# Reading and turning the weights beside the first group's order, on one core

## The chip, the cores and the metric

The kernel runs on one core of one Trainium2 chip. The metric is the time of one execution on the device in microseconds (us); for the kernel before it is the median of three runs. One further execution was recorded by the hardware profiler; all durations of single instructions are from it. The engines are named as the profile names them: PE (matrix products; PEld is its loading of weights), DVE (vector), ACT (activation functions), POOL (GpSimd) and SP (here it issues the DMA transfers). An activation function is looked up in a table set; when the next function isn't in the set that is loaded, an ACT_TABLE_LOAD stands before it.

## The reference

128 graphs of 64 nodes with 128 features go through four graph layers, each with a residual and a layer norm followed by a ReLU in front. Cut to what matters:

```python
h = relu(layernorm(x));  x = x + L0(h, adj)   # edge filters from a Gaussian basis of the edge weight
h = relu(layernorm(x));  x = x + L1(h, adj)   # hyperbolic attention over the neighbours
h = relu(layernorm(x));  x = x + L2(h, adj)   # normalised adjacency, one weight
h = relu(layernorm(x));  x = x + L3(h, adj)   # mean of messages, then an update weight

# L0, for the nodes j that i is joined with
g  = exp(coeff * (e[i, j] - offsets)**2)              # 64 offsets
Wf = (ssp(g @ W1.T + b1) @ W2.T + b2) * A[i, j]       # ssp: softplus - ln 2
y  = sum_j (h @ Wa.T)[j] * Wf * A[i, j]
L0 = ssp(y @ Wd1.T + bd1) @ Wd2.T + bd2
# L1 uses W, b_lin, att_w1, att_b1, att_w2, att_b2, mlp_w1, mlp_b1, mlp_w2, mlp_b2; its bias is
hyp_bias = proj(tanh(|b_lin|) * b_lin / |b_lin|)
# L2 uses W, b; L3 uses W_msg, W_upd
```

About a quarter of the edges are there, each with a weight from 0.05 to 5.

## The kernel before

The graphs are worked on in 16 groups of eight. A group lies in four pairs; the two graphs of a pair share the 128 partitions. Seven stages make a group: `load` (x and the adjacency), `order` (the nodes are sorted by their number of neighbours, the adjacency is brought into that order, and for every node its neighbours are put into slots, as zeros and ones in the tile `oh`), `layer0`, `layer1_nodes`, `layer1_edges`, `rest1` (the rest of layer 1) and `rest2` (layers 2 and 3, and the store). The edges are worked on by slot: two blocks of 512 slots and one of 264 for each pair, which are the shapes 128x1024 and 128x528 in the profile (two graphs side by side).

The order of the instructions on PE, DVE, ACT and POOL is laid down by a planner in the program, the class `Weave`. Every stage is a generator (a stream); `yield on(engine, ...)` ends a step and says on which engine the next one begins, which buffers of a ring it takes, after which events, and under which table set of ACT ("log" holds Exp and Ln, "silu" holds Silu and Tanh). The planner has its own estimate of each instruction's duration (`about`, line 785). It picks, of the streams that could begin within 0.05 us of the earliest on that engine, the one with the smallest key; the key is the stream's rank (2 x group + the stage's due time, in the last lines of `sparse_stack`) plus a number from the table `LATE` (line 808), one number for each step of each kind of stream. An instruction on these four engines is issued in the order in which the planner came to it, and each engine's queue is in order. The table sets are asked for in a loop outside the streams, with `preload_act_table_set`, first of all "log". SP is not in this order; transfers that wait for nothing go out in the order of the calls.

Small results on PE go to one PSUM bank, the ring "sm" (one buffer); the edge products go to "big" (three buffers). The order of a group needs "sm" for a chain of steps: two products into the counts of nodes with more neighbours, then x in the new order, the adjacency turned twice, its running count, and beside them the transposed h and its product with Wa, which gives `rf`.

Ahead of the weave, in plain program order, stand the constants and the weights (lines 999 to 1155). The helper `weight_t` (line 1067) reads a weight into a room, turns it on PE through "sm" and copies it out on DVE. The rooms come from `raw_tile` (line 991) and alternate between two tiles, e1 and e2, so that a read has to wait until the turn two before it has been done. The bias of layer 1 is computed with Sqrt and Tanh on ACT. The last of it is the message weight, whose two halves are turned and multiplied with the update weight. Since these instructions come first in the program, those of PE come first in PE's queue too; DVE's first instructions of `order` lie between those of the weights.

```python
    def raw_tile():
        name = f"e{1 + len(raws) % 2}"
...
    def transposed(src, dst):
        ps = psm.tile([P, 512], F32, name="sm", tag="sm")
        T.transpose(ps[:, :P], src, ident)
        V.tensor_copy(dst, ps[:, :P])
```

In the profile nearly all instructions have line 849, where the planner's helper issues them, so they are told apart by the names of their tiles: `e` with `ident` is a weight being turned, `e` with `w1T` and `ex` with `w2T` are layer 0's edge products, `ex<-big` is an Exp and `ex<-ex` the Ln after it, `hbn` is the bias, `oh` the slots of the order, `va` the edge weights in slots.

Of the kernel before, what the change touches and what calls it, by code (L numbers as in the profile page):

```python
# [11 lines left out]
F32 = mybir.dt.float32  # L12
U32 = mybir.dt.uint32
I32 = mybir.dt.int32
# [6 lines left out]
NP = 4  # L21
# [763 lines left out]
def about(engine, op, args, kw):  # L785
# [14 lines left out]
    if engine == ACT:  # L800
# [8 lines left out]
    "attention": (0, 3.75),  # L809
    "coefs_of": (2.5, 0, -0.25),  # L810
    "coefs_of2": (2.5,),
    "duo": (4, 4.25),
    "duo2": (0, 3.5, -1.5),
    "filter_of": (1.75, 3.5, 0.25, -0.75, 0, -2.25),
    "filter_of2": (-3.75, 3.5, 0, 4.5, -2.5),
    "layer1_edges": (0, 0, 0, -3),
    "layer1_nodes": (-2.25, 0, 0, 0, 0, 4.5, 0, 4.25, 1.75, 0, 0, 0, 0, 0, 3.5, 0.5, 0, 0, 0, 0, 0,
        0, 0, 0, -1.5, 0, 0, 0, 0, -3.25, 0, 0, 0, 0, 0, 0, -0.5, 0, 0, 0, 0, 0, 0, 3, 0, 0, 3),
    "neighbours": (-0.5, -2),
    "neighbours2": (3.5,),  # L820
    "one_minus_z": (-1.5,),
    "order": (0, 0, -2.25, 0, 0, 0, 4.25, 3.25, 0, -2, 0, 1.75, 0, 2.25, 0, 0, 1.75, 0, 6, -2.25),
    "product_with_h": (0, 2.5),
    "rest1": (0, 0, 0, -3.75, 0, 0, 0, 1, 0, -3.25, 0, 0, 0, 0, -0.5, -2, 0, 0, 0, 0, 0, 0, -1.25),
    "rest2": (0, 0, 0, 0, 0, 0, 0, 0, 0, 0, 0, -3.75, 0, 2, 0, 2.75, 0, 0, 0, 0, 3.5, 0, 0, 0, 0, 0,
        0, 0, 1),
    "rows": (1.25, -2.75),
    "rows2": (1.75, -0.25),
    "scores_of": (0.75, 0, -1.75, -0.5),
    "scores_of2": (0, -1.25),  # L830
    "squares": (2,),
    "squares2": (0, 2.25),
# [38 lines left out]
class Weave:  # L871
# [18 lines left out]
    def add(self, gen, rank=None, tail=False):  # L890
        rank = self.now.rank if rank is None else rank
        self.streams.append(Stream(gen, self.now.t if self.now else 0.0, rank, tail))

# [69 lines left out]
def sparse_stack(ctx: ExitStack, tc: tile.TileContext, ins, out: bass.AP, flag):  # L963
# [25 lines left out]
    raws = []  # L989

    def raw_tile():

        name = f"e{1 + len(raws) % 2}"
        raws.append(dense.tile([P, NP, N], F32, name=name, tag=name))
        return raws[-1].rearrange("q p n -> q (p n)")[:, 0:P]

# [30 lines left out]
    tri = raw_tile()  # L1027
# [14 lines left out]
    for c, blocks in enumerate(BLOCKS):  # L1042
        at = OFFS[c]
        for k, r0, n, k0 in blocks:
            ki = edge.tile([P, 1024], I32, name="ex", tag="ex", bufs=3)
            G.iota(ki[:, 0:k * n].rearrange("q (n k) -> q n k", n=n), [[0, n], [1, k]], base=k0 - 128,
                   channel_multiplier=0)
            V.tensor_copy(slot_k[:, at:at + k * n], ki[:, 0:k * n])
            V.tensor_copy(slot_r[:, at:at + k * n].rearrange("q (n k) -> q n k", n=n),
                          bl(ident2[:, r0:r0 + n], k))  # L1050
            at += k * n
# [11 lines left out]
    def transposed(src, dst):  # L1063
        ps = psm.tile([P, 512], F32, name="sm", tag="sm")
        T.transpose(ps[:, :P], src, ident)
        V.tensor_copy(dst, ps[:, :P])

    def weight_t(ap, name, dst=None):

        raw = raw_tile()  # L1070
        nc.sync.dma_start(out=raw, in_=ap)
        if dst is None:
            dst = const.tile([P, P], F32, name=name)
        transposed(raw, dst)
        return dst


    w1raw = raw_tile()
    nc.sync.dma_start(out=w1raw[:, 0:NG], in_=ins["L0_gnn_W1"])
    nc.sync.dma_start(out=w1raw[:, NG:P], in_=ins["L0_gnn_W1"])  # L1080
    w1T = const.tile([P, P], F32, name="w1T")
    transposed(w1raw, w1T)


    b1 = column("L0_gnn_b1")
    bound = const.tile([P, 1], F32, name="bound")
    V.tensor_scalar(w1raw[:, 0:NG], w1raw[:, 0:NG], 0.0, None, ALU.max)
    V.tensor_reduce(bound, w1raw[:, 0:NG], AX.X, ALU.add)
    V.tensor_tensor(bound, bound, b1, ALU.add)
    waT = weight_t(ins["L0_gnn_Wa"], "waT")  # L1090
    wd1T = weight_t(ins["L0_gnn_Wd1"], "wd1T")
    bd1 = column("L0_gnn_bd1")
    wd2T = weight_t(ins["L0_gnn_Wd2"], "wd2T")
    w2T = weight_t(ins["L0_gnn_W2"], "w2T")

    b2s = column("L0_gnn_b2")
    ps = psm.tile([P, 512], F32, name="sm", tag="sm")
    T.matmul(ps[:, 0:1], lhsT=w2T, rhs=nln2[:, 0:1], start=True, stop=True)
    V.tensor_tensor(b2s, ps[:, 0:1], b2s, ALU.add)
    bd2s = row("L0_gnn_bd2")  # L1100
    ps = psm.tile([P, 512], F32, name="sm", tag="sm")
    T.matmul(ps[:, :P], lhsT=nln2, rhs=wd2T, start=True, stop=True)
    V.tensor_tensor(bd2s, ps[:, :P], bd2s, ALU.add)


    wlinT = weight_t(ins["L1_gnn_W"], "wlinT")
    attT = const.tile([P, 2 * P], F32, name="attT")
    weight_t(ins["L1_gnn_att_w1"][:, P:2 * P], None, attT[:, 0:P])
    weight_t(ins["L1_gnn_att_w1"][:, 0:P], None, attT[:, P:2 * P])
    ab1 = column("L1_gnn_att_b1")  # L1110
    hab2 = const.tile([P, 1], F32, name="hab2")
    nc.sync.dma_start(out=hab2, in_=ins["L1_gnn_att_b2"].partition_broadcast(P))
    V.tensor_scalar(hab2, hab2, 0.5, None, ALU.mult)
    aw2 = const.tile([P, 1], F32, name="aw2")
    nc.sync.dma_start(out=aw2, in_=ins["L1_gnn_att_w2"].rearrange("o d -> d o"))
    aw2b = const.tile([P, N], F32, name="aw2b")
    V.tensor_scalar(aw2b, ones[:, 0:N], aw2, None, ALU.mult)
    m1aT = weight_t(ins["L1_gnn_mlp_w1"][:, 0:P], "m1aT")
    m1bT = weight_t(ins["L1_gnn_mlp_w1"][:, P:2 * P], "m1bT")
    mb1 = column("L1_gnn_mlp_b1")  # L1120
    m2T = weight_t(ins["L1_gnn_mlp_w2"], "m2T")
    mb2 = row("L1_gnn_mlp_b2")


    hb = row("L1_gnn_b_lin")
    hb2 = raw_tile()
    hbn = const.tile([P, 4], F32, name="hbn")
    V.tensor_tensor(hb2, hb, hb, ALU.mult)
    V.tensor_reduce(hbn[:, 0:1], hb2, AX.X, ALU.add)
    V.tensor_scalar(hbn[:, 0:1], hbn[:, 0:1], MIN_NORM2, None, ALU.max)  # L1130
    S.activation(hbn[:, 0:1], hbn[:, 0:1], AF.Sqrt)
    S.activation(hbn[:, 1:2], hbn[:, 0:1], AF.Tanh)
    V.tensor_scalar(hbn[:, 1:2], hbn[:, 1:2], MAXNORM, None, ALU.min)
    V.reciprocal(hbn[:, 2:3], hbn[:, 0:1])
    V.tensor_tensor(hbn[:, 1:2], hbn[:, 1:2], hbn[:, 2:3], ALU.mult)
    V.tensor_scalar(hb, hb, hbn[:, 1:2], None, ALU.mult)
    V.tensor_tensor(hb2, hb, hb, ALU.mult)
    hby2 = const.tile([P, 1], F32, name="hby2")
    V.tensor_reduce(hby2, hb2, AX.X, ALU.add)


    w2g = const.tile([P, P], F32, name="w2g")
    nc.sync.dma_start(out=w2g, in_=ins["L2_gnn_W"])
    b2g = row("L2_gnn_b")

    wupd = const.tile([P, 2, P], F32, name="wupd")
    nc.sync.dma_start(out=wupd, in_=ins["L3_gnn_W_upd"].rearrange("(s d) u -> d s u", s=2))
    wsu, wru = (const.tile([P, P], F32, name=n) for n in ("wsu", "wru"))
    for k, dst in enumerate((wsu, wru)):
        raw, rawT = (raw_tile() for _ in range(2))  # L1150
        nc.sync.dma_start(out=raw, in_=ins["L3_gnn_W_msg"][k * P:k * P + P, :])
        transposed(raw, rawT)
        ps = psm.tile([P, 512], F32, name="sm", tag="sm")
        T.matmul(ps[:, :P], lhsT=rawT, rhs=wupd[:, 1, :], start=True, stop=True)
        V.tensor_copy(dst, ps[:, :P])
# [185 lines left out]
    def load(g, st):  # L1341
        yield on(DVE, "x", "adj")
        x = st["x"] = pers.tile([P, NP, D], F32, name="x", tag="x")
        adj = st["adj"] = pers.tile([P, NP, N], F32, name="adj", tag="adj", bufs=5)
        gs = slice(2 * NP * g, 2 * NP * (g + 1))
        nc.sync.dma_start(out=adj, in_=adj_d[gs].rearrange("(p b) i j -> (b i) p j", b=2))
        nc.sync.dma_start(out=x, in_=x_d[gs].rearrange("(p b) i d -> (b i) p d", b=2))
        st["x_used"], st["adj_used"] = w.token("x"), w.token("adj")
        w.now.t += 5
        w.event("load", g)  # L1350

    def order(g, st):
# [31 lines left out]
        def normed_x():  # L1384
# [11 lines left out]
            yield on(POOL)  # L1396
# [8 lines left out]
            yield on(PE, "sm")  # L1405
# [34 lines left out]
        for c in range(3):  # L1440
            for at, k, r0, n in blocks_of(c):
                yield on(DVE)
# [26 lines left out]
    def layer0(g, st):  # L1469

        yield on(DVE, "ys", after=prior(("order", g), ("layer0", g - 1), ("va1", g - 2)))
# [139 lines left out]
    def layer1_nodes(g, st):  # L1611


        yield on(PE, "sm", "a0", "a1", after=prior(("layer0", g), ("nodes", g - 1)))
# [58 lines left out]
        def product_with_bias():  # L1673
            yield on(POOL, after=[("n2", g)])
# [403 lines left out]
    def rest2(g, st):  # L2078

        yield on(PE, "sm", after=prior(("rest1", g), ("rest2", g - 1)))  # L2080
# [122 lines left out]
    with tc.manual_schedule(engines={E.Activation, E.PE, E.DVE, E.Pool}):  # L2203
        for g in range(GROUPS):
# [53 lines left out]
```

## Time and profile before

| | |
|---|---|
| median of 3 runs | 2149.32 us (2148.49 to 2150.37) |
| the profiled execution | 2152.3 us, of which its span 2150.5 |
| busy over the span | PE 1826.5 (85%), DVE 1832.9 (85%), ACT 1671.5 (78%), POOL 369.7 (17%) |
| mean granted clock of PE | 0.941 of full |
| table loads on ACT | 87, 111.6 us |
| first matmul of the first group's order | 36.20 us |
| stores of the groups 0 and 9 | 489.2 and 1579.4 us |

The span is cut into 40 slices of 53.8 us each; a digit is the busy share of an engine in a slice, in tenths.

```profile
## 2 busy tenths in 40 slices
PE   3767989898999989898999989898999989896773
DVE  4448889899999989899999989899999999887752
ACT  1968787979879797979879797979879797985541
PEclk9988999999999999999999999999999999998775
DMA  2000000000000000000000000000000000000000
```

PE and DVE are at 8 or 9 tenths from the fifth slice on and fall off in the last four. The DMA engines do next to nothing after the first slice.

### The profile page before, as it was taken

The numbers are of one execution on the slowest core, as the hardware profiler recorded it, in microseconds if no ns is written. First come the engines' busy times: TensorE is split into PE (matmuls) and PEld (weight loads), VectorE is DVE, ScalarE is ACT, GpSimd is POOL, SyncE is SP. The second block draws the span as 40 slices with busy tenths as digits, with TensorE's granted clock in tenths as the row PEclk, the third lists the DMA queues.
The fourth block names the chain that finished last, engine by engine and source line by source line (L and its number), as shares of the span: only waits on it lengthen the run. The fifth ranks groups of instructions, "written<-read, shape, count | busy, mean of one in ns | idle before, by whom it ended". The sixth has DMA issues, their size and how long they took to land.

```text
span 2150.5 us, 32066 instructions
## 1 busy us (share of the span) xinstructions
PE 1826.5 (85%) x11223; PEld 873.5 (41%) x11223; DVE 1832.9 (85%) x4829; ACT 1671.5 (78%) x3385; POOL 369.7 (17%) x362
## 2 busy tenths in 40 slices
PE   3767989898999989898999989898999989896773
PEld 2223333443444444443444444443444444433342
DVE  4448889899999989899999989899999999887752
ACT  1968787979879797979879797979879797985541
POOL 1000101122120212122120212222130212202121
PEclk9988999999999999999999999999999999998775
DMA  2000000000000000000000000000000000000000
GB/s 52 5 0 6 1 6 1 1 6 8 6 8 6 8 6 8 1 6 8 6 8 6 8 6 8 1 6 8 6 8 1 8 1 6 1 1 6 5 1 12
DMA packets 29532, 13.95 MB, mean 6 GB/s; under 512 B 10544, under 2 KB 29360, under 8 KB 29360
## 3 DMA queue, kind: packets, MB, share of 16 engines
q1 hardware_dynamic: 29360, 11.80, 2.1%
q8 instruction: 90, 1.47, 0.3%
q14 instruction: 82, 0.67, 0.1%
HBM read 7.61 MB, written 4.19 MB: 5 GB/s over the span
## 4 chain that ended last, share of the span: by engine, by line
PE 41%; ACT 31%; DVE 22%; issue 4%; DMA 1%; POOL 0%; SPq 0%; DVEq 0%; ACTq 0%; POOLq 0%
PE big L849 29%; PE sm L849 9%; ACT ex L849 9%; ACT e L849 5%; DVE va L849 4%; ACT ra L849 4%; PE sl L849 4%; ACT n L849 3%; DVE oh L849 3%; DVE ex L849 2%; DVE ah L849 2%; DVE y L849 2%; ACT va L849 2%; ACT L849 2%; ACT th L849 1%
## 5 line engine op out<-in xcount | busy, mean ns | idle before, releaser
L849 PE MATMUL big<-ex,w2T 128*128 128x512 f32 (+1 forms) x768 | 328.5, 553 | 41.3 <-ACT ex L849 35.0
L849 PE MATMUL big<-e,w1T 64*128 64x512 f32 (+1 forms) x768 | 205.3, 635 | 57.2 <-ACT e L849 52.6
L849 ACT ACTIVATE ex<-big,c_L_gnn_att_b 128x1024 f32<-128x1024 f32 (+1 forms) x192 | 183.3, 968 | 78.0 <-PE big L849 77.4
L849 DVE SCALAR_TENSOR_TENSOR ex<-big,c_L_gnn_b,ra 128x1024 f32<-128x1024 f32 x128 | 163.8, 1280 | 67.8 <-PE big L849 55.6
L849 PEld LDWEIGHTS big<-ex,w2T 128*128 128x128 f32 x768 | 131.2, 190 | 215.7 <-ACT ex L849 93.0
L849 ACT ACTIVATE ex<-big,c_L_gnn_b 128x1024 f32<-128x1024 f32 (+1 forms) x192 | 184.6, 978 | 43.9 <-PE big L849 43.6
L849 PE MATMUL big<-va,U 64*128 64x512 f32 (+1 forms) x768 | 184.7, 558 | 31.8 <-DVE va L849 31.6
L849 PE MATMUL big<-va,a 64*128 64x512 f32 (+1 forms) x768 | 185.5, 579 | 10.3 <-DVE two L849 4.3
L849 PE MATMUL sl<-ex,aw2b 128*64 128x512 f32 (+1 forms) x768 | 180.7, 549 | 8.4 <-ACT th L849 4.5
L849 ACT ACTIVATE ra<-big 128x528 f32<-128x528 f32 (+1 forms) x192 | 167.3, 884 | 17.7 <-PE big L849 17.0
L849 ACT ACTIVATE ex<-ex 128x1024 f32<-128x1024 f32 (+1 forms) x192 | 175.6, 924 | 0.9
L849 DVE TENSOR_REDUCE y<-ex 128x128 f32<-128x1024 f32 x128 | 155.1, 1212 | 0.8
L849 POOL TENSOR_TENSOR k_r<-k_r,exp 128x4 f32<-128x4 f32 x32 | 47.5, 1484 | 580.4 <-DVE k_r L849 568.7
L849 ACT ACTIVATE th<-sl,hab 128x512 f32<-128x512 f32 (+1 forms) x192 | 118.1, 615 | 37.0 <-PE sl L849 35.2
L849 PE MATMUL big<-slot_r,Sx 64*128 64x512 bf16 (+1 forms) x1152 | 137.4, 343 | 0.0
L849 PEld LDWEIGHTS big<-e,w1T 64*128 64x128 f32 x768 | 69.4, 205 | 155.6 <-ACT e L849 65.2
L849 ACT ACTIVATE va<-va,sr 128x512 f32<-128x512 f32 (+1 forms) x192 | 122.5, 649 | 9.0 <-DVE va L849 9.0
L849 PE MATMUL big<-oh,pqs 64*64 64x512 bf16 (+1 forms) x1152 | 122.8, 347 | 0.0
L849 ACT ACT_TABLE_LOAD x87 | 111.6, 1283 | 2.2 <-PEq L2246 0.7
L849 DVE COPY_PREDICATED va<-slot_r,big 128x1024 f32<-128x1024 uint16 (+1 forms) x96 | 106.6, 1111 | 5.3 <-PE big L849 5.1
L849 DVE TENSOR_TENSOR va<-oh,adjT 128x1024 f32<-128x1024 bf16 (+6 forms) x160 | 103.6, 697 | 5.7 <-ACT va L849 4.9
L849 DVE TENSOR_TENSOR oh<-pos,slot_k 128x2048 bf16<-128x2048 bf16 (+6 forms) x128 | 107.7, 849 | 0.2
(470 smaller groups left out, 3799.6 us busy)
## 6 DMA issues: line engine op xcount, KB each, us to landing
x<-in_x_dram SPq DMA_DIRECT2D x16, 256.0 KB, 2.9
out_dram<-v SPq DMA_DIRECT2D x16, 256.0 KB, 2.3
adj<-in_adj_dram SPq DMA_DIRECT2D x16, 128.0 KB, 2.3
e<-in_L_gnn_mlp_w_dram SPq DMA_DIRECT2D x3, 64.0 KB, 1.8
wupd<-in_L_gnn_W_upd_dram SPq DMA_DIRECT2D x1, 128.0 KB, 5.8
e<-in_L_gnn_Wd_dram SPq DMA_DIRECT2D x2, 64.0 KB, 2.9
e<-in_L_gnn_W_dram SPq DMA_DIRECT2D x2, 64.0 KB, 1.8
e<-in_L_gnn_att_w_dram SPq DMA_DIRECT2D x2, 64.0 KB, 1.8
```

The source lines that it names most:

```text
L849: return f(*args, **kw)
```

## The change

The weights of the layers are no longer read and turned ahead of the weave. Four streams with rank -10 do it inside: `slots_ranks` (the slot tables that the order compares with), `weights0` (layer 0), `weights1` (layer 1 and its bias, with one stream `turned_from` for each of its six turns) and `weights2` (layers 2 and 3, after the events "weights1" and "bias1"). The rooms are now twelve halves of six tiles that later stages use, each for one weight, and for layer 3 a tile of four rooms; no read waits for another turn. The single numbers (columns and rows) are still read ahead. The turns take "sm" as a ring. Stages wait for events: the order for "wa" and "weights0" (at the steps that use them) and for "slots"; `layer0` for "weights0", `layer1_nodes` for "weights1", its product with the bias for "bias1", `rest2` for "weights2". The bias is computed with Ln, Exp and Exp under the table set "log", and Tanh under "silu", in place of Sqrt, Tanh and a reciprocal. The table LATE has other numbers throughout, and entries for the new streams. The diff, with the table and some renamed declarations cut:

```diff
 LATE = {
-    "attention": (0, 3.75),
+    "attention": (0, -0.5),
...
+    "slots_ranks": (3.5, 0, 4.75),
+    "turned_from": (3.5,),
+    "weights_of": (-3,),
...
+    def wait(self, us):
+        self.now.t += us
...
-    raws = []
-    def raw_tile():
-        name = f"e{1 + len(raws) % 2}"
-        raws.append(dense.tile([P, NP, N], F32, name=name, tag=name))
-        return raws[-1].rearrange("q p n -> q (p n)")[:, 0:P]
+    rooms = [(name, k) for name in ("e2", "e4", "bR", "rt", "rs", "mask", "e1") for k in range(2)]
+    def raw_tile():
+        name, k = rooms.pop(0)
+        if k == 0:
+            raw_tile.last = dense.tile([P, NP, N], F32, name=name, tag=name)
+        return raw_tile.last.rearrange("q p n -> q (p n)")[:, P * k:P * k + P]
...
+    def turned(raw, dst):
+        yield on(PE, "sm")
+        ps = psm.tile([P, 512], F32, name="sm", tag="sm")
+        T.transpose(ps[:, :P], raw, ident)
+        yield on(DVE)
+        V.tensor_copy(dst, ps[:, :P])
+        w.release("sm")
...
+    def weights0():
+        yield on(DVE)
+        w1raw = raw_of(ins["L0_gnn_W1"], ins["L0_gnn_W1"])
+        raw = {n: raw_of(ins["L0_gnn_" + n]) for n in ("Wa", "Wd2", "W2", "Wd1")}
+        w.wait(5)
+        yield from turned(raw["Wa"], waT)
+        w.event("wa")
+        yield from turned(w1raw, w1T)
...
+        yield from turned(raw["W2"], w2T)
+        ps = yield from product(w2T, nln2[:, 0:1], 1)
+        V.tensor_tensor(b2s, ps, b2s, ALU.add)
+        yield from turned(raw["Wd2"], wd2T)
+        ps = yield from product(nln2, wd2T, P)
+        V.tensor_tensor(bd2s, ps, bd2s, ALU.add)
+        yield from turned(raw["Wd1"], wd1T)
+        w.event("weights0")
...
+    def weights1():
+        yield on(DVE)
...
+            w.add(turned_from(raw_of(ap), dst))
...
-    S.activation(hbn[:, 0:1], hbn[:, 0:1], AF.Sqrt)
-    S.activation(hbn[:, 1:2], hbn[:, 0:1], AF.Tanh)
...
-    V.reciprocal(hbn[:, 2:3], hbn[:, 0:1])
...
+        yield on(ACT, table="log")
+        act(hbn[:, 1:2], hbn[:, 0:1], AF.Ln)
+        act(hbn[:, 0:1], hbn[:, 1:2], AF.Exp, scale=0.5)
+        act(hbn[:, 2:3], hbn[:, 1:2], AF.Exp, scale=-0.5)
+        yield on(ACT, table="silu")
+        act(hbn[:, 1:2], hbn[:, 0:1], AF.Tanh)
...
+        w.event("bias1")
...
+    def weights2():
+        yield on(DVE, after=[("weights1",), ("bias1",)])
+        nc.sync.dma_start(out=w2g, in_=ins["L2_gnn_W"])
+        nc.sync.dma_start(out=wupd, in_=ins["L3_gnn_W_upd"].rearrange("(s d) u -> d s u", s=2))
+        room = wide.tile([P, NP, D], F32, name="w3", tag="w3")
...
+            yield from turned(raws[2 * k], raws[2 * k + 1])
+            ps = yield from product(raws[2 * k + 1], wupd[:, 1, :], P)
+            V.tensor_copy(dst, ps)
+        w.event("weights2")
...
+        for stream in (slots_ranks, weights0, weights1, weights2):
+            w.add(stream(), -10)
         for g in range(GROUPS):
```

## The prediction

> **What bounds the kernel now.** I read the page first, and from it only the forty slices: the first slice has PE 3 and ACT 1, the fifth is the first in which PE stands at 9, and the last four fall away. So there is a start-up, a long even middle and a drain. Next I asked for the busy time by stage, with cuts at the first matmul of the first group's order (36.2 us), its first edge weights (51.8) and its first layer-0 sum (136.5).
>
> ```profile
> core 0: us, PE busy (x) PEld busy (x) DVE busy (x) ACT busy (x) POOL busy (x), PEclk, DMA share, GB/s
> 0.00:36.20 36.20, 8.91 (x21) 4.41 (x22) 12.72 (x63) 4.25 (x5) 5.20 (x26) 1.00 0.29 69
> 36.20:51.80 15.60, 8.33 (x63) 6.17 (x62) 9.57 (x21) 2.51 (x5) 3.56 (x4) 1.00 0.06 18
> 51.80:136.50 84.70, 58.96 (x244) 22.25 (x245) 38.97 (x59) 79.40 (x86) 0.00 (x0) 0.92 0.01 3
> 400.00:1800.00 1400.00, 1271.27 (x8072) 605.38 (x8070) 1307.89 (x3440) 1182.57 (x2426) 264.06 (x235) 0.98 0.02 6
> ```
>
> In the middle (last row) DVE is busy 93%, PE 91%, ACT 84%; the change takes no instruction out of it. In the first 36 us nothing is busy for more than a third. In the third stage ACT is busy 94%, PE 70%, DVE 46%. The chain of waits shows who owns the first stage: from 13.76 us, when the first adjacency has landed and DVE works on it, the chain follows PE's twelve transposes and four products of weights, with a bias computation between, before the order's own matmul:
>
> ```profile
> 13.76 0.29 DVE o L849
> ...
> 34.17 0.49 PE sm L849
> 34.68 0.30 DVE e L849
> 35.03 0.81 PE sm L849 x2
> 35.86 0.30 DVE wru L849
> 36.20 0.60 PE sm L849 x2
> 36.83 0.43 DVE o L849
> ```
>
> DVE has done its share of the order (the row pos from ident and degs) at 16.25; PE gets to it at 36.20, because PE's queue is in order and the weights stand in it. What fills ACT in the third stage is in the timeline of ACT:
>
> ```profile
> 29.69 1.28 ACT L849 ACT_TABLE_LOAD   x1
> 30.99 0.20 ACT L849 ACTIVATE hbn<-hbn 128x1 f32<-128x1 f32 x1
> ...
> 128.18 1.28 ACT L849 ACT_TABLE_LOAD   x1
> 129.47 1.12 ACT L849 ACTIVATE ex<-big,c_L_gnn_b 128x1024 f32<-128x1024 f32 x1
> 130.61 1.28 ACT L849 ACT_TABLE_LOAD   x1
> 131.90 1.06 ACT L849 ACTIVATE ex<-ex 128x1024 f32<-128x1024 f32 x1
> 132.86 1.00 ACT L849 ACTIVATE ra<-big 128x1024 f32<-128x1024 f32 x1
> 133.89 2.57 ACT L849 ACT_TABLE_LOAD   x2
> ...
> 167.53 0.20 ACT L849 ACTIVATE nn<-nn 128x8 f32<-128x8 f32 x1
> 167.76 0.21 ACT L849 ACTIVATE rr<-nn 128x8 f32<-128x8 f32 x1
> ```
>
> Between an Exp (ex from big) and the Ln after it (ex from ex) stands a table load, and another before the next Exp. After the pair at 133.89, which the program asks for itself, Ln and Exp follow each other without one (167.53, 167.76: Ln, Exp). The groups of ACT in this stage count 23 loads, 29.5 us, mean 1283 ns; less the two asked for, 21 are the alternation. Its cause, by the order in the trace: the program's own load of the set with both functions stands at 0.72 us, and the Tanh of the bias brought another set at 29.69; nobody asked for the joint set again until 133.89.
>
> **The start.** Removed from the front of PE's queue: everything before 36.20. Added: the same turns, in the weave, beside the order. I cost it in three terms.
>
> First, when the adjacency lands. Before, 15 transfers are issued ahead of it on SP, about 0.47 us apart; the issue is at 8.01, DVE uses it at 13.76, 5.7 later. After, 11 columns and rows and 12 weight loads are called ahead of it, since the weight streams have rank -10 and the load -6: eight more, 8 x 0.47 = 3.8. So 13.8 + 3.8 = 17.5 us; bounds 13.8 (SP takes it earlier) and 20 (transfers also queue on each other: the row loads took 3.6 to 5.7). DVE's share is 16.25 - 13.76 = 2.5: PE can begin the order at 20.0, 16.2 before 36.2.
>
> Second, the order's chain itself, from its first matmul to the first edge weights: 36.20 to 51.88, 15.7 us, unchanged.
>
> Third, what the turns put between. Layer 0 and layer 1 need 11 transposes and two products, each of which holds the one small PSUM bank ("sm") that the order uses too. A round, from 23.00 to 23.87, is 0.86 us; 11 x 0.86 and the two products (0.8 and 1.18) make 11.4 us. In time, all of it could lie before 20.0; but the queue is laid by a plan that thinks weights and adjacency are there at 4 or 5 us, so only three or four rounds come first. Of the other nine or ten, one fits where DVE computes between the order's first two matmul steps (1.3 us) and two or three beside the 6.3 us in which DVE writes the eight blocks of oh. That leaves some 5.5 on the path: 5.5 x 0.86 = 4.7. Bounds: none (0) and all (11.4).
>
> Sum: 20.0 + 15.7 + 4.7 = 40.4 instead of 51.9: 11.5 us saved. With all bounds bad: 22.5 + 15.7 + 11.4 = 49.6, 2 saved; with all good: 16.3 + 15.7 = 32, 20 saved.
>
> What is queued behind the new waits: the DVE instructions on hab and aw stand near the front of DVE's manual queue as before and wait for a transfer landing near 8 us; nothing urgent is behind them then. Layer 0's wait for the first weights ends before its other wait, the order's oh, unless the plan puts Wd1 late. The slot tables (3.5 us of DVE from 8.7 to 12.8) lie ahead of the adjacency in either kernel. The waits of the layer-1 nodes for the second weights and of the mlp bias product for the bias come 80 us later. The turns for layer 3 (two transposes, two products, 3.4 us of PE and DVE) now come after the bias, near the end of the first layer 0, where PE is under half busy (136 to 160 us); I take them at 0, at most 3.4. Their consumer, rest2 of group 0, ends at 489 us. SP is in order too, and its loads of x wait for PE; if it put the loads of these weights behind one, PE would stand at their transposes, for the 2 to 5 us of a load at the least. They need nothing but room, so I expect them early.
>
> **The tables.** The bias's Sqrt, Tanh and reciprocal become Ln, two Exp and, under the silu set, Tanh. Outside the plan no ACT function is left that could change the set, so the joint set loaded first stays through the first layer 0, and the 21 loads go. The Tanh falls between the two loads at 133.89, behind which ACT idles 5.5 us before the first nodes: its 0.2 is hidden.
>
> Two rules of the Trainium skill must be weighed here. In the trace the load at 130.61 begins 0.02 after the Exp has ended, and the Ln at 131.90 follows 0.01 after the load: 1.31 us a switch, 21 x 1.31 = 27.5. "ScalarE: Activation LUTs", in What ACT_TABLE_LOAD costs, has a load of 1283 ns, which the trace confirms, and a drain of 1380 besides, 2.66 in all: 21 x 2.66 = 56 us, more than the stage's ACT time leaves room for (79.4 - 56 = 23, while the activations alone sum to 49.9). The row decides. The other speaks against the change: "ScalarE activation tables: per-element evaluation and per-set limits", in Table sets in the compiler and the runtime, says loads are placed per block by the greedy longest run. By that, a run of Exp and Ln would get one load for both, and a forgotten set would cost 1.3 once; this program's rows show 21 instead, so here the set kept is the one last asked for, and what restores the joint set ends the alternation. If I misread that, the loads stay (a rival below).
>
> ACT's 79.4 shrink to 49.9. What is late next is PE: 58.96 busy, of which some 4.5 are slow clock (the four w2T matmuls at 73.20 took 3.78 us at a granted 0.50, at 98.88 1.98 at 1.00), so about 54.5. With the busiest engine at 85%, less than the middle's 93% because one group alone fills and drains here, the stage takes 54.5 / 0.85 = 64.1 instead of 84.7: 20 us saved. Bounds: PE at 75% gives 72.7 (12 saved); above, the 27.5 of the loads.
>
> **The order found anew** changes the keys by which the plan breaks ties, in all sixteen groups. No row tells its sign. From the stores of groups 0 and 9 (489.2 and 1579.4) a group takes 121.1 us, and with DVE at 93% there is little to win; I bound it by 1% each way, 1.2 us a group in 12 full groups, 15 us, and take 0.
>
> **Sum.** 11.5 + 20 = 31.5. The profiled execution took 2152.3, 2150.5 of span and 1.8 around; it becomes 2120.8. The median of before is 3.0 lower, so 2149.3 - 31.5 = 2117.8: I say 2118.
>
> **The rivals.**
> - The tables come out, the start does not (rounds ahead of the order, a late adjacency): 2149.3 - 20 - 2 = 2127. For it: rank -10 beats the order's keys wherever both are ready. 0.12.
> - The loads stay, some other ACT step having changed the set or the pass placing them by function: 2149.3 - 11.5 = 2138. Against it: no load between Ln and Exp after 133.89. 0.08.
> - The new order also gains 1% or more in the middle: 2118 - 15 = 2103. 0.20. For it: PE, DVE and ACT all leave 7 to 16% idle, in many small waits.
> - Slower: the new order loses in the middle. DVE at 93% is the engine that would show it, as waits for PE or ACT. It decides from 31.5 / 13 = 2.4 us a group, 2% of 121.1; at 3% (3.6 x 13 = 47) the time is 2165. 0.05.
> - The forecast, with the middle within 0.6%: 2118, from 2107 to 2129. 0.55.
>
> **How the numbers follow.** A measurement of this kernel can tell about 0.2%, 4 us, from no change. Faster by more has all cases but the slower one and a sliver of the "loads stay" case with a bad middle: 0.93; within, 0.02; slower 0.05. The range leaves out the slower case, half of the case of a better middle at its far end and the worst of the loads: 2096 to 2137.
>
> **What the profile after would show.** First order matmul near 20 us, first edge weights near 40, and small transposes of weights between; if that start is at 49, my third term was wrong. Table loads in the first layer 0: none; 64 in all instead of 87 (the Sqrt's and the Tanh's own go too). ACT below 85% and PE above 80% in that stage, which lasts about 64 us; if it lasts over 73, a wait between PE and ACT (three big PSUM buffers) has taken the loads' place. Store to store 121 us in the middle: if it is under 120 or over 122.3, the new order did that, and my 0 for it was wrong.

## The result and the profile after

The changed kernel takes 2121.03 us (median of four runs, 2119.59 to 2125.34) against 2149.85 for the kernel before in the same comparison. The ratio is 0.9868, with a 95% interval from 0.9853 to 0.9884: 29 us less. The profiled execution took 2121.5, with a span of 2119.6. The forecast was 2118, in a range from 2096 to 2137. The sum came out right; two of its terms were wrong, in opposite directions, and the experiments below are mostly about these.

Busy time by stage in the changed kernel, with cuts at the first matmul of the order (20.85 us), the first edge weights (39.24) and the first matmul of y with wd1T (93.77), and the even middle. In the kernel before, the last of these events is at 135.92, 0.6 us ahead of the cut at 136.50 that the prediction took:

```profile
core 0: us, PE busy (x) PEld busy (x) DVE busy (x) ACT busy (x) POOL busy (x), PEclk, DMA share, GB/s
0.00:20.85 20.85, 4.65 (x11) 2.30 (x12) 8.99 (x49) 1.78 (x4) 5.25 (x26) 1.00 0.50 120
20.85:39.24 18.39, 10.23 (x67) 6.87 (x66) 10.74 (x26) 2.52 (x5) 3.57 (x4) 1.00 0.05 15
39.24:93.77 54.53, 49.38 (x244) 20.22 (x245) 38.51 (x57) 48.42 (x64) 0.00 (x0) 1.00 0.02 6
400.00:1800.00 1400.00, 1258.60 (x8049) 598.26 (x8049) 1323.13 (x3426) 1172.43 (x2397) 265.77 (x243) 0.98 0.02 6
```

The first stage is 15 us shorter, the second 3 longer, the third 29 shorter (84.0 before, between the same two events). In the third, ACT has fallen from 79 to 48 us and is at 89%; PE is the busier engine, at 91%. The column PEclk can't be read for the first stages: the trace's clock records begin at 44.80 us here and at 62.05 in the kernel before, and ahead of them the view prints 1.00. The timeline of ACT at the end of that stage has the Tanh of the bias between the two loads that the program asks for, and an idle stretch after them:

```profile
90.72 1.05 ACT L853 ACTIVATE ex<-ex 128x1024 f32<-128x1024 f32 x1
92.06 1.02 ACT L853 ACTIVATE ra<-big 128x1024 f32<-128x1024 f32 x1 [0.30 <-PE big L853]
93.11 1.28 ACT L853 ACT_TABLE_LOAD   x1
94.40 0.20 ACT L853 ACTIVATE hbn<-hbn 128x1 f32<-128x1 f32 x1
94.62 1.28 ACT L853 ACT_TABLE_LOAD   x1
100.85 1.29 ACT L853 ACTIVATE a<-a 128x512 f32<-128x512 f32 x2 [4.95 <-DVE a L853]
```

There is no other load from the first edge weights on to here; in the whole run there are 64 instead of 87.

The chain of waits at the start of the changed kernel. It no longer runs through the adjacency: from 8.76 us it is the first weight's transfer, then turns, then the order with more turns between:

```profile
8.76 2.76 DMA bR<-in_L_gnn_W_dram
11.66 0.46 PE sm L853
...
20.85 0.60 PE sm L853 x2
21.48 0.43 DVE o L853
21.94 0.43 DVE places L853
22.39 0.42 DVE perm L853
22.82 0.21 DVE wd1T L853
23.07 0.49 PE sm L853
23.58 0.30 DVE m1aT L853
23.93 0.49 PE sm L853
24.44 0.30 DVE m1bT L853
24.79 0.49 PE sm L853
25.30 0.30 DVE m2T L853
25.65 2.00 PE sm L853 x16
```

perm is ready at 22.81, and the order's next matmul starts at 25.65. Four turns stand between the order's two steps on PE, one of layer 0 (wd1T) and three of layer 1: the first lies beside DVE's work, the other three keep the order waiting for 2.8 us.

Where the lead over the kernel before is, event by event, from the starts of these instructions in the two traces:

| event | before | after | lead |
|---|---|---|---|
| first edge weights of group 0 | 51.8 | 39.2 | 12.6 |
| y with wd1T, group 0 (layer 0 done) | 135.9 | 93.8 | 42.1 |
| the same, group 1 | 246.5 | 207.1 | 39.4 |
| last edge product of layer 1 (va with U), group 0 | 271.2 | 231.7 | 39.5 |
| the same, group 3 | 627.6 | 593.1 | 34.5 |
| the same, group 15 | 2057.9 | 2024.5 | 33.4 |
| store of group 15 | 2139.4 | 2108.5 | 30.9 |

A lead of 42 us after the first layer 0 has become 31 at the end. The middle is not where it goes: the stores of the groups 1 and 9 are 969.6 us apart in both kernels, 121.2 a group.

### The profile page after: what moved, and what is told of

Read it like the earlier page. It is cut to its first block, busy times and chain, and to the rows that moved or that the text cites. A ratio compares the mean times of both kernels' runs of the same rounds, so it can differ in the third digit from the quotient of the medians.

```text
span 2119.6 us, 31941 instructions
## 1 busy us (share of the span) xinstructions
PE 1806.3 (85%) x11223; PEld 866.0 (41%) x11223; DVE 1847.9 (87%) x4828; ACT 1641.1 (77%) x3364; POOL 364.5 (17%) x362
## 4 chain that ended last, share of the span: by engine, by line
PE 37%; DVE 36%; ACT 19%; issue 7%; POOL 0%; SPq 0%; DMA 0%; DVEq 0%; ACTq 0%; POOLq 0%
PE big L853 25%; PE sm L853 9%; ACT ex L853 6%; DVE va L853 5%; DVE ex L853 4%; PE sl L853 4%; ACT e L853 4%; DVE th L853 4%; DVE y L853 2%; ACT ra L853 2%; DVE ah L853 2%; DVE v L853 2%; ACT n L853 2%; DVE att L853 2%; DVE oh L853 1%
## 5 line engine op out<-in xcount | busy, mean ns | idle before, releaser
L853 PE MATMUL big<-ex,w2T 128*128 128x512 f32 (+1 forms) x768 | 320.2, 542 | 41.8 <-ACT ex L853 20.6
L853 PE MATMUL big<-va,a 64*128 64x512 f32 (+1 forms) x768 | 181.1, 568 | 10.7 <-DVE k_s L853 3.8
L853 POOL TENSOR_TENSOR k_r<-k_r,exp 128x4 f32<-128x4 f32 x32 | 32.4, 1013 | 583.1 <-DVE k_r L853 578.7
L853 DVE SCALAR_TENSOR_TENSOR th<-th,oh 128x1024 f32<-128x1024 f32 (+1 forms) x80 | 99.2, 1240 | 13.8 <-ACT th L853 13.8
L853 ACT ACTIVATE e<-e 128x1024 f32<-128x1024 f32 (+2 forms) x144 | 106.7, 752 | 1.1
L853 PE MATMUL big<-va,ones 64*64 64x512 f32 (+1 forms) x768 | 97.4, 559 | 11.0 <-DVE va L853 11.0
```

The lines of the kernel that those rows point to most:

```text
L853: return f(*args, **kw)
```

## The experiments

Twelve kernels were run; each ratio is to runs of the kernel before on the same chip.

### Which of the three parts does what

The change has three parts that can be had one by one: the **tables** (no loads in the first layer 0), the **start** (weights in the weave) and the **order** (the new numbers of LATE). Two values of each make eight kernels; two of them are the kernels compared here. Three more edits give the other six:

```diff
# "tables only": the kernel before, with (the tanh of n as 1 - 2 / (exp(2 n) + 1), on DVE)
-    S.activation(hbn[:, 0:1], hbn[:, 0:1], AF.Sqrt)
-    S.activation(hbn[:, 1:2], hbn[:, 0:1], AF.Tanh)
+    S.activation(hbn[:, 1:2], hbn[:, 0:1], AF.Ln)
+    S.activation(hbn[:, 0:1], hbn[:, 1:2], AF.Exp, scale=0.5)
+    S.activation(hbn[:, 2:3], hbn[:, 1:2], AF.Exp, scale=-0.5)
+    S.activation(hbn[:, 3:4], hbn[:, 0:1], AF.Exp, scale=2.0)
...
# "start only": the changed kernel, with
-        act(hbn[:, 1:2], hbn[:, 0:1], AF.Ln)
-        act(hbn[:, 0:1], hbn[:, 1:2], AF.Exp, scale=0.5)
-        act(hbn[:, 2:3], hbn[:, 1:2], AF.Exp, scale=-0.5)
+        act(hbn[:, 0:1], hbn[:, 0:1], AF.Sqrt)
+        act(hbn[:, 3:4], hbn[:, 0:1], AF.Tanh)
...
# "old order" and "new order": the table LATE of the kernel before, or of the changed one
```

At this point I had a theory A (the 11 us are lost in the filling of the pipeline, whatever the order) and two rivals, B (the new numbers lose them) and C (the new numbers gain).

New code with the old order: 

> The changed kernel with the numbers of the old table LATE (the new streams have none). The changed kernel is 42 us ahead at the end of the first layer 0 (first matmul of y with wd1T at 93.8 instead of 135.9) and only 31 at the end. Theory A: the 11 us are lost in the filling and draining of the pipeline whatever the order's fine numbers are: 2121 within 5 us, the lead at the end of group 0's layer 0 about 40. Theory B: the new numbers lose it: with the old ones the lead is kept, 2110 to 2113. Theory C: the new numbers gain: 2125 to 2135 here.

Old code with the new order: 

> The kernel before with the new table LATE. Theory A: 2150 within 5 us, store to store in the middle 121.2 as before. Theory B: slower, 2157 to 2162. Theory C: faster, 2135 to 2145.

Tables only, old order: 

> The kernel before with its bias computed by Ln and Exp alone (the tanh by Exp and a reciprocal on DVE), so that the joint table set stays; the start is left as it was. All theories: no table load in the first layer 0, which lasts about 55 us from the first edge weights to the first wd1T matmul instead of 84, as in the changed kernel; so wd1T at about 107. Theory A1, later stages keep about three quarters of any lead: 2150 - 0.74 x 29.5 = 2128. Theory A2, the first 11 us of any lead are lost to something fixed: 2150 - 18 = 2132.

Start only, new order: 

> The changed kernel with Sqrt and a Tanh (whose result is not used) in place of Ln and the two Exp ahead of the first layer 0, so that the other table set is the one loaded and the 21 loads come back; all else as in the changed kernel. All theories: first edge weights at 39, the first layer 0 about 84 us long. Theory A1: 2150 - 0.74 x 12.6 = 2141. Theory A2: 2148. If the two parts were not additive, the layer 0 here would be shorter than 80.

Tables only, new order (run later): 

> The kernel before with the bias by Ln and Exp alone, and the new numbers of LATE. With the old numbers this edit gave 2120.7. Theory N (the new numbers cost some 7 us whatever else is there, after the first layer 0): 2124 to 2128, and the end of group 0's layer 0 no later than with the old numbers. Rival I (the numbers were fitted to a start with the weights in it and cost 7 only in another one): 2118 to 2121.

Start only, old order (run later): 

> The changed kernel with the 21 loads brought back by a Sqrt and a Tanh, and the old numbers of LATE. The start is worth 6.8 us between the two kernels without the loads and with the old numbers (2120.7 and 2113.9). If it adds to the loads: 2150 - 7 = 2143. If the loads in the first layer 0 swallow it or double it: outside 2139 to 2147.

Measured, median us and ratio with its interval:

| | old order | new order |
|---|---|---|
| neither | 2149.9 (the kernel before) | 2147.99, 0.9993 (0.9985 to 1.0001) |
| start | 2141.31, 0.9957 (0.9944 to 0.9971) | 2143.89, 0.9976 (0.9969 to 0.9983) |
| tables | 2120.74, 0.9870 (0.9856 to 0.9884) | 2130.74, 0.9903 (0.9888 to 0.9918) |
| tables and start | 2113.94, 0.9832 (0.9820 to 0.9845) | 2121.03, 0.9868 (the changed kernel) |

The tables alone give 29.2 us with the old order, as much as the whole change. PE's 11223 matmuls stand in the same order in the traces of the two kernels. Here is the first layer 0 from its first edge weights to its first wd1T matmul, in the kernel before and in the one with the tables only:

```profile
core 0: us, PE busy (x) PEld busy (x) DVE busy (x) ACT busy (x) POOL busy (x), PEclk, DMA share, GB/s
51.88:135.90 84.02, 58.36 (x243) 21.91 (x244) 38.63 (x58) 78.84 (x86) 0.00 (x0) 0.93 0.01 3
```

```profile
core 0: us, PE busy (x) PEld busy (x) DVE busy (x) ACT busy (x) POOL busy (x), PEclk, DMA share, GB/s
50.90:105.50 54.60, 49.30 (x243) 20.05 (x244) 38.52 (x58) 49.32 (x64) 0.00 (x0) 1.00 0.02 5
```

54.6 us against 84.0: 29.4 less in the stage and 29.2 less in the time. ACT is idle for 5.2 us of the stage before and for 5.3 with the tables, so the gain is ACT time that is no longer needed. A lead is not eaten by the filling of the pipeline: A, with both of its variants (2128 and 2132), fell, and so did C. The start gives 6.8 with the old order and no loads, 8.6 with the loads (there it adds, as forecast), 9.7 and 4.1 with the new order. The new order costs 7.1 in the changed kernel and 10.0 where only the tables were changed; with the loads in place it is 2.6 worse with the start, where the intervals still overlap, and 1.9 better without, which is within the noise. B holds where the loads are gone: there the new order costs 7 us. Its figure for the new code, 2110 to 2113, was 1 us low, and that for the old code, 2157 or more, was wrong.

The traces show what hides the loss there. With the new order 17 of the alternating loads stand in the first layer 0 and not 21 (83 loads in all instead of 87, in both kernels that have them), which is 4 x 1.31 = 5.2 us less for ACT. In the old code wd1T of group 0 comes 5.9 us earlier with the new order (130.1, 135.9), and the last store yet 0.5 later (2139.9, 2139.4). From that wd1T to the last store the new order takes longer in all four pairs, by 6.4 us with neither part, 5.2 with the start, 14.5 with the tables and 7.4 with both (one profile each; with the tables the two profiled runs lie 5.6 us further apart than the medians). It also means that "start only" brought back 21 loads with the old order, but 17 with the new one. With the tables alone the new numbers lose even more than I gave them (2130.7, expected 2124 to 2128), so they weren't good only beside the new start, the rival there.

For the new code, the traces with the two orders show the loss in three places. The last edge product of group 0 comes 1.8 us earlier (231.7, 233.5), that of group 3 2.3 later (593.1, 590.8), so 4.1 are lost in the groups 1 to 3; in the last group it is 3.2 later (2024.5, 2021.3), and from there to the last store the drain takes 84.0 instead of 81.6. The middle is 121.2 us a group in both.

### The turns for layer 3, and turns moved behind the order

In the run of the new code with the old order, the turns for layer 3 (the two halves of the message weight, each turned and multiplied) stand in the serial part of group 0's layer-1 nodes. The timeline of PE there (w is the room of the message weight):

```profile
102.89 0.48 PE L849 MATMUL sm<-ident,w 128*128 128x128 f32 x1 [0.92 <-DVE a L849]
105.60 0.80 PE L849 MATMUL sm<-wupd,w 128*128 128x128 f32 x2 [2.24 <-DVE w L849]
106.78 2.08 PE L849 MATMUL sm<-wd2T,a 128*128 128x128 f32 x8 [0.39 <-DVE wsu L849]
109.71 0.48 PE L849 MATMUL sm<-ident,w 128*128 128x128 f32 x1 [0.85 <-DVE x L849]
111.07 0.80 PE L849 MATMUL sm<-wupd,w 128*128 128x128 f32 x2 [0.88 <-DVE w L849]
```

```diff
     def weights2():
-        yield on(DVE, after=[("weights1",), ("bias1",)])
+        yield on(DVE, after=[("weights1",), ("bias1",), ("va1", 0)])
```

With the old order: 

> The changed kernel with the old numbers of LATE, and the turns for layer 3 (weights2) held until the first group's layer-1 edges have been begun. In the run with the old numbers they stood in the serial chain of the first layer-1 nodes: from the first wd1T matmul to the next group's first w1T matmul 34.0 us, against 29.3 where only the tables were changed. Theory: those 4.7 us come back, but for about 1 that the bias on DVE costs: the stretch is 30 to 31 us, the time 2110 to 2111 instead of 2113.9. Rival: the stretch is set by the slow matmul clock and the nodes' own chain, and the turns lay in its gaps: 2114.

Measured: 2289.6, ratio 1.067. The stretch that the edit was about did get shorter, from 34.0 us (95.55 to 129.51) to 31.8 (95.85 to 127.69), 2.2 of the 4.7 us that the theory had; but the planner's later choices fell out otherwise (PE's matmuls stand in another order in 8561 of 11223 places), and from there on a group takes 134.6 us (last edge products of the groups 2 and 13: 491.5 and 1972.5). Busy time of that kernel's middle:

```profile
core 0: us, PE busy (x) PEld busy (x) DVE busy (x) ACT busy (x) POOL busy (x), PEclk, DMA share, GB/s
400.00:1800.00 1400.00, 1164.82 (x7166) 553.76 (x7162) 1190.13 (x3056) 1057.41 (x2141) 226.25 (x215) 0.95 0.02 5
```

The same work goes through at a DVE share of 85% instead of 94%, with nothing added to it. The total says nothing about the turns.

With the new order: 

> The changed kernel as it is, new numbers too, with only the turns for layer 3 held until the first group's layer-1 edges. If their cost adds to that of the new numbers: 3 to 4 us less than 2121, 2117 to 2118. If the new order, which does all of the first nodes before the next layer 0, has room for them: 2121.

Measured: 2121.42, ratio 0.9877 (0.9863 to 0.9891), and from wd1T of group 0 to that of group 1 113.2 us, against 113.4 without the edit. The first of these turns moves from 100.4 to 211.0 us, and nothing is gained: in the changed kernel itself the turns for layer 3 lie in gaps.

The same, with the other turns held back too:

```diff
     def turned_from(raw, dst):
-        w.wait(4)
+        yield on(DVE, after=[("rf", 0)])
...
-        yield on(DVE)
+        yield on(DVE, after=[("soft", 0)])
         V.tensor_scalar(hbn[:, 1:2], hbn[:, 1:2], MAXNORM, None, ALU.min)
```

> As layer3_late, and the six turns of layer 1 held until rf of the first group has been written, the rest of the bias until the first nodes' softplus. In the changed kernel four turns (3.4 us) stand between the order's two first steps on PE, where DVE needs 1.3 us, and six more before it. Theory: first edge weights at 36 to 37 instead of 39.8, and 1 us less in the nodes: 2107 to 2109. Rival: the adjacency lands at 17, so that the order can't begin sooner, and the turns cost as much beside the first edge weights: as layer3_late, within 2 us.

Measured: 2297.1, 1.068, with 134.3 us a group again. Only the start can be read, against the run before: DVE uses the adjacency at 14.6, the order's first matmul comes at 16.2 instead of 24.1, the first edge weights at 37.9 instead of 39.6, wd1T at 92.8 instead of 95.8. The rival's reason is wrong (the adjacency doesn't land at 17), and the theory's 36 to 37 was not reached.

The new numbers for the early streams only: 

> The changed kernel with the new numbers for the streams of order, layer 0, layer-1 nodes and weights, and the old ones for the layer-1 edges, rest1 and rest2. The new numbers as a whole cost 7 us in this code (2121 against 2113.9). If they lose it in the filling (groups 1 to 3, where the ends of the edge products fall back by 4 us): 2118 to 2121. If they lose it in the later stages (rest of group 0 stored 6 us later after its edges, 2.4 us more in the drain): 2114 to 2116.

Measured: 2299.2, 1.071; a group takes 134.6 us here as well. Which of the new numbers lose the 7 us stays open: a mixture of the two tables is a third order, not a part of either.

### The transfers in another order

SP is not planned, so the calls of its transfers can be moved without a change in the planned order: PE's matmuls stand in the same order in the traces with and without the edit. Their order here: three small inputs that DVE waits for first, the weights as they are turned, the few columns and rows that the turns need among them, the adjacency, then the rest.

```diff
+    read("hab2", "aw2", "L1_gnn_b_lin", "lin0", "Wa0", "W10", "W11", "L0_gnn_b1", "att10", "W20",
+         "L0_gnn_b2", "att00", "Wd20", "L0_gnn_bd2", "Wd10", "mlp00", "mlp10", "mlp20", "L0_gnn_bd1")
...
     def weights2():
         yield on(DVE, after=[("weights1",), ("bias1",)])
+        read("L1_gnn_att_b1", "L1_gnn_mlp_b1", "L1_gnn_mlp_b2", "L2_gnn_b")
```

With the old order: 

> The changed kernel with the old numbers of LATE, and the transfers on SP in another order of calls (SP isn't planned, so the order on the other engines stays): first the three small inputs that DVE waits for, then the weights in the order in which they are turned, then the adjacency, and last the columns and rows that nobody needs early. The turns began at 11.7 us, when the first weight had landed. Theory: they begin near 5, the order's first matmul comes at 18 to 19 instead of about 23, first edge weights at 35 to 36 instead of 39.8; some 60% of it stays: 2110 to 2112 instead of 2113.9. Rival: the adjacency lands later for the weights in front of it, and nothing moves: 2114.

With the new order: 

> As reads_first, with the new numbers of LATE: against 2121. The order's first matmul comes after only eight rounds here, and DVE has its share of the order done at 18.6: at most 2 us earlier, first edge weights at 37 instead of 39.2, so 2119 to 2120.

Measured: 2109.10, ratio 0.9808 (0.9794 to 0.9821), with the old order, and 2115.25, 0.9835 (0.9819 to 0.9851), with the new one. PE at the start of the first of these:

```profile
5.01 0.45 PE L849 MATMUL sm<-ident,bR 128*128 128x128 f32 x1 [5.01 <-DMA bR<-in_L_gnn_W_dram]
7.73 0.48 PE L849 MATMUL sm<-ident,e 128*128 128x128 f32 x1 [2.27 <-DVE wlinT L849]
...
18.15 0.47 PE L849 MATMUL sm<-ident,mask 128*128 128x128 f32 x1 [0.39 <-DVE m1bT L849]
19.60 0.37 PE L849 MATMUL sm<-last_d,bones_b 128*128 128x256 bf16 x1 [0.97 <-DVE m2T L849]
19.76 0.42 PE L849 MATMUL sm<-pos,bones 128*128 128x256 bf16 x1
21.66 1.97 PE L849 MATMUL sm<-x,perm 64*64 64x128 f32 x16 [1.48 <-issue]
```

The turns begin at 5.0 instead of 11.6, the order at 19.6 instead of 24.2, and the first edge weights come at 35.1 instead of 39.8. By the medians all of these 4.7 us are kept (2113.9 to 2109.1), more than the 60% that I had put down; but the intervals of the two ratios just touch, so that the share is not settled. The new order gains 5.8, where I had at most 2 (first edge weights at 34.1, expected at 37). This is the fastest version, 41 us ahead of the kernel before and 12 ahead of the changed one (0.9808 and 0.9868, with intervals that don't meet).

## Why the prediction held, point by point

- **The adjacency** was put at 17.5; DVE uses it at 17.24. That is luck: the transfer is issued at 12.40 and has landed 2.4 us later (5.7 in the kernel before), at 14.8. DVE comes to it only then because the slot tables and the copies of the turns stand ahead in its queue, the last at 17.16, behind a product that PE does at 16.57. **The order's first matmul** was put at 20.0; it is at 20.85. It waits there for a turn and not for DVE (pos is done at 18.57).
- **The turns in between** were put at 4.7 us of a path of 20.4 from the order's first matmul to the first edge weights; the path is 18.4, 2.7 longer than without turns. The plan put nine rounds ahead of the order and four behind its first step, not three or four ahead. First edge weights: forecast 40.4, measured 39.24.
- **Where that lead goes.** I wrote 11.5 us saved and counted it in full. The first edge weights do come 12.6 us earlier, but the start is worth 6.8 in the end with the old order and 9.7 with the new one, by the runs without the loads. Of the 11.1 us between the two kernels at the first edge weights (50.9, 39.8; old order) 10.0 are left at wd1T of group 0 (105.5, 95.5) and 3.7 at wd1T of group 1 (212.4, 208.7): most of the loss is in the nodes of group 0, where the layer-3 turns and the rest of the bias now stand. Moving the turns gave 2.2 us of that stretch back, so "I take them at 0, at most 3.4" was too low there, but for its bound; in the changed kernel moving them brought nothing. The rest of the loss is not assigned. A rival is left: the granted clock is 0.50 for 23.9 us from 100.4 on in these nodes, and for 13.7 us (from 114.5) in the kernel with the tables only. These positions are from one profile each and don't sum to the medians exactly.
- **The tables** were forecast at 20 us and gave 29. This is the term that was mis-sized, and by more than its upper bound of 27.5. The step that failed: "58.96 busy, of which some 4.5 are slow clock", so 54.5, "at 85%". Measured with the tables only: PE's busy time in the stage falls from 58.4 to 49.3 us for the same matmuls, and PE is at 90% of the stage (91 in the changed kernel). Of the 9.6 us between the forecast stage (64.1) and that of the changed kernel (54.5), 6.0 come from the busy time (49.4 us at 85% would make 58.1) and 3.6 from the share. The 4.5 came from rows at a granted clock of 0.50. That clock is on record from 68.87 to 79.11, with PE busy 8.43, and from 133.72 on, with 2.18; half of it is 5.3 us, so this part was about right. What was left out lies, for 2.0 us, ahead of the first clock record, at 62.05: PE is at half speed there too, as four matmuls of one kind ahead of it and behind it show:

```profile
57.85 2.08 PE L849 MATMUL big<-e,w1T 64*128 64x512 f32 x4 [1.08 <-ACT e L849]
62.16 1.02 PE L849 MATMUL big<-e,w1T 64*128 64x512 f32 x4
```

  With the tables only the first record of full clock is at 56.49, the first of these groups takes 1.13 us, and the four rows of matmuls that the kernel before has from there to 62.05 take 2.0 us less. The remaining 1.8 us of the 9.1 are not assigned. It is the loads that bring the clock down: in the four kernels with loads the mean granted clock of this stage is 0.90 to 0.93 by the profile, in the ten without it is 1.00. Which of PE's stops do it is not shown, for from 79.11 to 133.72 the clock is at 1.00 with the loads in place. The page "TensorE: Matmul & The Clock Gate" of the Trainium skill, in Part 1: The HAM clock gate, has the array throttled by default and activity releasing it; the trace agrees, with half speed at the start, to 62.05 before and to 56.49 with the tables only. This is also why the removed instructions alone were no bound. The last w2T group ahead of wd1T took 3.12 us at the lowered clock (at 133.01) and takes 1.98 without the loads: 1.1 of the 1.9 us beyond 27.5.
- **The table rules.** A switch costs 1.31 us by the row, and the stage confirms it: 21 such are 27.5 of its 29.4 us; the 56 of the page's load and drain are out of the question. And the alternation ends, in either code, when the set that the program asked for is not displaced: the rule of the longest run does not describe this program.
- **The order found anew** was put at 0 within 15. It is a loss of 7 us in the changed code. The forecast that the middle stays at 121 held (121.2); the loss is mostly in the first four groups and in the drain, which I had not looked at.
- **The sum.** 29 for the tables, 7 for the start, 7 lost to the order: 29. The forecast had 20, 11.5 and 0: 31.5. It was right within 3 us because 9 too few and 12 too many met, and that is luck. The mechanisms were the two I named; their sizes were not.
- **The signs.** No alternating load, 64 loads in all, the order's first matmul near 20 and the first edge weights near 40 came as forecast. The stage was to last 64 us with ACT below 85%; it lasts 54.5, with ACT at 89%. Two rows were read too low: in the first 36 us DVE is busy for 12.72 of 36.20, 35%, and not under a third, and from 136 to 160 PE is busy for 12.10 of 24.00, half the time, at a granted clock of 0.64.
- **The rivals.** That the loads stay was wrong (none left). "The tables come out, the start does not", 2127, is wrong as to its cause but came close in the number. That the new order gains in the middle is wrong (121.2 us a group in both kernels). That it makes the kernel slower had the right sign for that part; it was 7 us, where it needed 31.

## What to carry to other kernels

When a removed instruction made other engines wait, cost the stage from what its next engine needs at full speed, and don't bound the gain by the removed time: here 27.5 us of table loads were worth 29.4. Look where the clock records of a profile begin before its clock column is used. Where a greedy planner lays the order, any edit of a stream is also a new order: test it with both tables of tie-breaks, read single stretches instead of totals, and change things that the planner doesn't see (here the order of the transfers) when a small part is to be measured. A change of three parts is worth its eight corners, for the sum may hide one part that loses.

## What the runs showed that I had not expected

The new order moves POOL's two 128x512 operations of a group beside DVE's writing of the slots (oh), and POOL then takes two to three times as long for them. One of them before and after (busy us, mean ns):

```profile
L849 POOL TENSOR_TENSOR xp<-xp,r_L_gnn_bd 128x512 f32<-128x512 f32 x16 | 20.3, 1267 | 1.1
```

```profile
L853 POOL TENSOR_TENSOR xp<-xp,r_L_gnn_bd 128x512 f32<-128x512 f32 x16 | 47.0, 2937 | 1.3
```

And a product of two 128x4 tiles on DVE, between two blocks of oh, took a median of 155 ns before and of 1002 ns after (min, median, max):

```profile
L849 DVE TENSOR_TENSOR rb<-rb,un x16: 129/155/164, 357.6 to 2084.7; 128x4 f32<-128x4 f32 x16
```

```profile
L853 DVE TENSOR_TENSOR rb<-rb,un x16: 147/1002/1004, 310.3 to 2053.8; 128x4 f32<-128x4 f32 x16
```

One such place in the changed kernel, on both engines:

```profile
795.84 2.26 DVE L853 TENSOR_TENSOR oh<-pos,slot_k 128x2048 bf16<-128x2048 bf16 x1
796.48 2.52 POOL L853 TENSOR_TENSOR a<-xp,o_mv 128x512 f32<-128x512 f32 x1
798.02 1.00 DVE L853 TENSOR_TENSOR rb<-rb,un 128x4 f32<-128x4 f32 x1
799.03 2.25 DVE L853 TENSOR_TENSOR oh<-pos,slot_k 128x2048 bf16<-128x2048 bf16 x1
799.08 3.34 POOL L853 TENSOR_TENSOR xp<-xp,r_L_gnn_bd 128x512 f32<-128x512 f32 x1
```

The blocks of oh take 2.26 and 2.25 us, no longer than one in the kernel before with no POOL operation beside it (2.28 at 941.26). POOL's operation `a<-xp,o_mv`, a median of 1.16 us in the kernel before, outlasts the first of them, and the small product ends with POOL's operation, at 799.0. So POOL is held up beside the large block, and DVE in the small product. The old order has the like of it: another POOL operation stands there, a 128x4 `un<-un` that takes 2.15 us (at 950.25; 0.32 at 981.61, beside no such block), and the block of oh beside it takes 2.59. POOL's busy time over the span is 369.7 us before and 364.5 after.

With the old order in the new code the small product is at 156 ns again. DVE is busy 15 us more over the span (1847.9 against 1832.9), 10 of them in this product, and yet a group takes 121.2 us in both, so that DVE's busy time, at a share of 93%, does not set the period alone. What does was not tried.
